# Attention by blocks of queries, with each block's end run as steps inside the next block

## The chip, the cores and the metric

One core of one Trainium2 chip. The metric is the time of one execution on the device, in microseconds (us). Each kernel was timed in several executions beside executions of the kernel before on the same chip. Later calls ran on different chips, so times are compared within a call, or by their ratio to the kernel before. A ratio is the mean time of one kernel's fast runs over the mean time of the other's fast runs of the same rounds, so it isn't quite the ratio of the medians that stand beside it. All timed runs of this study were of the fast state; a kernel with one single execution has no state that can be judged, and is marked so.

## The reference

Four images of 48 x 48 tokens with 128 channels go through two layers. The first is a selective scan (group norm, a projection, a 3 x 3 depthwise convolution with silu, scans in four directions, a gate and a projection). The second is what this change is about: attention over the 2304 tokens of an image, and a spectral convolution (`_stu`) of the normalised result.

```python
def _L1_attn_ref(x):
    attn = jnp.einsum('bnd,bmd->bnm', x / TEMPERATURE, x)      # TEMPERATURE = 1
    attn = jax.nn.softmax(attn, axis=-1)
    return jnp.einsum('bnm,bmd->bnd', attn, x)
...
t = _to_tokens(x)                                    # (4, 2304, 128)
t = t + _L1_attn_ref(_ln_t(t))
t = t + _L1_ffn_ref(_ln_t(t), ...)                   # spectral convolutions of the second norm
```

## The kernel before

The four images are handled one after the other ("batches" 0 to 3). Each has three stages:

- the **scans**: 768 of them, VectorE's and GpSimd's work, and beside them on TensorE the spectral convolutions (`cv`) of the batch before;
- the **turn**: the scans' epilogue, then the attention, with the next batch's prologue (projections `ip` on TensorE, 18 depthwise "taps" of 2.6 us on VectorE, silu on ScalarE) put between its steps;
- the **tail**, run as the first steps of the next batch's scans: the attention's result is turned, divided by the softmax's denominators, added to the tokens `T`, normalised into `u`, and stored for the convolutions. The convolutions can't start before it ends.

The attention goes over all keys, and for each over five chunks of queries, so that five accumulators end together. ScalarE's exponential also adds up the denominators:

```python
for i in range(NT + 1):                                        # 18 blocks of 128 keys
    nxt = pool.two.tile([P, L], F32, tag="e", ...) if i < NT else None
    for q, (lo, w) in enumerate(chunks):                       # 4 x 512 and 1 x 256 queries
        if i < NT:
            p = ps.pss.tile([P, 512], F32, tag="s", ...)
            nc.tensor.matmul(p[:, :w], xnT[:, i * P:(i + 1) * P], xnT[:, lo:lo + w], start=True, stop=True)
            nc.scalar.activation(nxt[:, lo:lo + w], p[:, :w], AF.Exp, bias=shift, accum_out=sm[:, i, q:q + 1])
        if i > 0:
            values(i - 1, e, q)
        yield
    e = nxt
```

The norm that closes the tail visits four engines' queues in turn, which matters below:

```python
def normed(x, d, eps, small, sq, name):
    ...
    nc.vector.tensor_tensor(d, x, s.unsqueeze(2).to_broadcast([k, m, C]), ALU.subtract)   # u <- T
    nc.scalar.activation(sq[:k], d, AF.Square)                                            # usq <- u
    yield
    nc.vector.tensor_reduce(v, sq[:k], AX.X, ALU.add)
    nc.vector.tensor_scalar(v, v, 1.0 / C, eps, ALU.mult, ALU.add)
    nc.gpsimd.tensor_tensor(v, v, mhalf[:k, :m], ALU.pow)                                 # ln_vu
    yield
    nc.vector.tensor_tensor(d, d, v.unsqueeze(2).to_broadcast([k, m, C]), ALU.mult)       # u <- u, ln_vu
```

Scans and convolutions are interleaved by a count of matmul columns. `more` puts convolutions down until their share of the columns has caught up with the scans' share; each of the tail's steps is booked in that count with 300 columns, 4500 in all:

```python
def more(share):
    while done[0] < share * total:         # total: the scans' own columns + work_cols
        cols = next(work, None)
        if cols is None:
            break
        done[0] += cols
...
TAIL_COLS = 300
TAIL_COLS_ALL = TAIL_COLS * (NM + 10)      # 4500
...
scans(b, *first, front, sp, ps, later(b - 1, held, ps), STU_COLS + TAIL_COLS_ALL)
```

## Time and profile before

| what | kernel before |
|---|---|
| time, median of 3 runs | 7205.91 us (7194.62 to 7206.78) |
| TensorE busy, share of the span | 88% |
| VectorE, GpSimd, ScalarE | 67%, 53%, 42% |
| mean granted clock of TensorE | 0.911 |

How to read it: TensorE bounds two of the three stages, and its 88% is an average over those and over two holes, the epilogue and the tail. The prediction shows the stretches. Two more lines are needed later. The first is from the page's table of groups: busy us and mean ns of one, then the idle time of the engine just ahead of them and what ended most of it.

```profile
L698 PE MATMUL s<-xnT 128*128 128x512 f32 (+1 forms) x720 | 340.3, 556 | 2.0 <-ACT e L699 2.0
```

The second is the largest entry of TensorE's waits in the first attention with prologue (1298 to 1470 us), a step of the scans' preparation: us in total, times, longest.

```profile
PE sp L395 <- ACT u L378: 2.0, 1, 2.0
```

So before, a score hardly ever waits for an exponential: 2.0 us in the whole program.

### The profile page before, as it was taken

To read this page: it belongs to the slowest core of one execution; us is meant where nothing else is said; L and a number is where in the kernel's file an instruction comes from. 1 tells how busy PE (TensorE), PEld (TensorE's weight loads), DVE (VectorE), ACT (ScalarE), POOL (GpSimd) and SP (SyncE) were. 2 spreads that over 40 slices of the span, in tenths; PEclk is the share of its full clock that TensorE was granted. 3 is DMA by queue.
4 is the path that set the end of the run, shared out by engine and by line. 5 is a ranking of instruction groups with operands and counts; after the bars stand their busy time and mean duration, and the time that the engine had idled before them with its cause. 6 is when DMAs were issued, how large, how long until landed. Compare 5 with 4: busy or idle time off the path is not lost. (4 is left out here: it accounts for less than half of the span.)

```text
span 7207.2 us, 79853 instructions
## 1 busy us (share of the span) xinstructions
PE 6362.3 (88%) x26760; PEld 3677.8 (51%) x26760; DVE 4834.5 (67%) x6045; ACT 3028.8 (42%) x5984; POOL 3837.3 (53%) x1795
## 2 busy tenths in 40 slices
PE   4777776868999998878999999778999999889999
PEld 2333333434555566534555556534555556547788
DVE  6899887467888876447888886447888887412111
ACT  3666664434444543334445543344444543231000
POOL 2888886046777775025677775215677776300000
PEclk7777777989999999889999999889999999789999
DMA  4555553056767676045767776126767777215545
GB/s 96 135 138 133 139 136 95 15 122 144 180 178 187 182 192 178 14 96 130 178 173 186 184 191 199 39 62 134 168 170 182 188 187 200 72 35 139 157 142 176
DMA packets 648924, 1019.14 MB, mean 141 GB/s; under 512 B 93850, under 2 KB 506650, under 8 KB 623779
## 3 DMA queue, kind: packets, MB, share of 16 engines
q1 hardware_dynamic: 642816, 1010.84, 54.6%
q8 instruction: 213, 3.49, 0.2%
q10 hardware_dynamic: 5698, 3.21, 0.2%
q14 instruction: 197, 1.61, 0.1%
HBM read 895.86 MB, written 117.84 MB: 141 GB/s over the span
## 5 line engine op out<-in xcount | busy, mean ns | idle before, releaser
L456 POOL TENSOR_TENSOR s<-s,bc 128x1536 f32<-128x1536 f32 x768 | 2645.9, 3446 | 259.3 <-DVE s L447 156.7
L447 DVE TENSOR_TENSOR_SCAN s<-dA,carry,s 128x384 f32<-128x384 f32 x2560 | 2437.8, 999 | 229.5 <-ACT dA L444 222.0
L444 ACT ACTIVATE dA<-rep,A 128x384 f32<-128x384 f32 x3072 | 1753.8, 584 | 991.4 <-DVE s L447 976.2
L948 PE MATMUL cv<-tt,u 128*128 128x256 f32 (+4 forms) x7680 | 1684.2, 359 | 84.5 <-DVE U L968 71.4
L948 PEld LDWEIGHTS cv<-tt,u 128*128 128x128 f32 (+1 forms) x7680 | 1276.5, 191 | 669.0 <-issue 298.6
L968 DVE TENSOR_TENSOR U<-cv,Q 128x256 f32<-128x256 f32 (+1 forms) x1280 | 490.8, 391 | 1116.9 <-PE cv L948 1100.3
L439 POOL TENSOR_TENSOR s<-rep,bc 128x1536 f32<-128x1536 f32 x288 | 993.9, 3451 | 98.1 <-DMA bc<-bcd 98.1
L948 PE MATMUL cv<-tt,us 128*128 128x256 f32 (+4 forms) x3840 | 870.1, 363 | 88.5 <-DVE U L968 39.4
L439 DVE TENSOR_TENSOR s<-rep,B 128x1536 f32<-128x1536 f32 x480 | 833.9, 1737 | 72.1 <-PE B L431 58.6
L464 PE MATMUL y<-s,csum 128*32 128x384 f32 x6144 | 718.2, 542 | 168.3 <-POOL s L456 155.1
L957 ACT COPY Q<-cv 128x256 f32<-128x256 f32 (+3 forms) x640 | 224.5, 351 | 1410.3 <-PE cv L948 1288.6
L948 PEld LDWEIGHTS cv<-tt,us 128*128 128x128 f32 (+1 forms) x3840 | 638.6, 192 | 342.9 <-issue 142.0
L1006 PE MATMUL pr<-U,G 128*128 128x512 f32 (+4 forms) x2048 | 733.9, 492 | 47.9 <-DMA G<-gd 43.3
L455 POOL COPY carry<-s 128x4 f32<-128x4 f32 x640 | 120.3, 188 | 1191.4 <-DVE s L447 1123.0
L447 DVE TENSOR_TENSOR_SCAN s<-dA,s 128x384 f32<-128x384 f32 x512 | 457.3, 939 | 52.1 <-ACT dA L444 48.7
L431 PE MATMUL B<-xd,spread 32*128 32x384 f32 x960 | 473.7, 575 | 18.8 <-DVE s L439 18.1
L1006 PEld LDWEIGHTS pr<-U,G 128*128 128x128 f32 x2048 | 348.3, 198 | 261.7 <-issue 174.9
L464 PEld LDWEIGHTS y<-s,csum 128*32 128x32 f32 x6144 | 126.0, 112 | 598.8 <-POOL s L456 294.4
L161 POOL TENSOR_TENSOR ln_vu<-ln_vu,mhalf 128x4 f32<-128x4 f32 (+1 forms) x20 | 20.1, 1005 | 762.2 <-DVE ln_vu L160 762.2
L699 ACT ACTIVATE e<-s,shift 128x512 f32<-128x512 f32 (+1 forms) x360 | 232.0, 644 | 304.8 <-PE s L698 303.8
L698 PE MATMUL s<-xnT 128*128 128x512 f32 (+1 forms) x720 | 340.3, 556 | 2.0 <-ACT e L699 2.0
L809 PE MATMUL G<-M,W 128*128 128x128 f32 (+2 forms) x768 | 237.7, 459 | 116.6 <-DMA M<-in_M_phi_plus 114.9
(165 smaller groups left out, 5055.5 us busy)
## 6 DMA issues: line engine op xcount, KB each, us to landing
rep<-dtdud SPq DMA_DIRECT2D x768, 384.0 KB, 7.8
tt<-fd SPq DMA_DIRECT2D x192, 577.0 KB, 4.1
bc<-bcd SPq DMA_DIRECT2D x2304, 48.0 KB, 3.8
tt<-fd SPq DMA_DIRECT2D x192, 513.0 KB, 4.1
tt<-fd SPq DMA_DIRECT2D x192, 385.0 KB, 4.0
dtdud<-re SPq DMA_DIRECT2D x768, 96.0 KB, 2.2
G<-gd SPq DMA_DIRECT2D x192, 256.0 KB, 4.8
tt<-fd SPq DMA_DIRECT2D x64, 514.0 KB, 5.4
```

The source lines that it names most:

```text
L431: nc.tensor.matmul(self.bt[:, :CS], spread[32:64, self.q].rearrange("p c j -> p (c j)"), self.ch.xd[32:64], start=True, stop=True)
L439: eng.tensor_tensor(s, self.ch.rep[self.h][:, 1], bt.unsqueeze(1).to_broadcast([P, G4, CS]), ALU.mult)
L444: nc.scalar.activation(dA[:, :CS], ch.rep[self.h][:, 0, g], AF.Exp, scale=A[:, ch.k, self.h * G4 + g, self.q:self.q + 1])
L447: nc.vector.tensor_tensor_scan(s, dA[:, CS - 1::-1] if ch.rev else dA[:, :CS], s, 0.0 if ch.first else carry[:, self.h, self.q, g:g + 1], ...
L456: nc.gpsimd.tensor_tensor(self.s, self.s, ch.bc[Q4 + self.q].unsqueeze(1).to_broadcast([P, G4, CS]), ALU.mult)
L464: nc.tensor.matmul(ch.y[g * DL:(g + 1) * DL, :CS], csum, self.s[:, g], start=(self.q == 0), stop=(self.q == Q4 - 1))
L698: nc.tensor.matmul(p[:, :w], xnT[:, i * P:(i + 1) * P], xnT[:, lo:lo + w], start=True, stop=True)
L699: nc.scalar.activation(nxt[:, lo:lo + w], p[:, :w], AF.Exp, bias=shift, accum_out=sm[:, i, q:q + 1])
L809: nc.tensor.matmul(p[:, :n] if j else p[:, NF - 1 - i], W[:, q if t else 0, i], M[t][:, i].unsqueeze(1).to_broadcast([P, n, C]) if j else ...
L948: nc.tensor.matmul(p2[:, :, at - first:], x, t[:kp, :, hi - 1 - at + J * P:end if end >= 0 else None:-1], start=(J == 0), stop=(J == nb - 1))
L968: nc.vector.tensor_tensor(dst, src, q, ALU.add)
L1006: nc.tensor.matmul(p[:, :, :v], Gs[n][:, q, x, :], U[n][:, 4 * q:4 * q + 4, :v], start=False, stop=(k == KF - 1 and q == 1 and v == w))
```

## The change

Its intent: let the attention finish a block of 512 queries at a time, so that the tail of a block can run as single steps inside the next block, and only one block's tail is left when the scans start. Parts:

1. Loops exchanged: blocks of queries in the order 0, 4, 1, 2, 3 outside, keys inside. Scores of a block can start as soon as pieces of `xnT` are kept, so they start within the epilogue.
2. The denominators: the last channel of the values' operand is set to 1, so the values matmul itself gives the sum of the exponentials there. The true last channel is got back as minus the sum of the others, since the rows of `xn` have mean 0.
3. Each block's tail is a generator, stepped once per attention step.
4. The tail and its 4500 columns leave the scans.

```diff
-    def attention(b, xn, xnT, oT, den, pool, ps):
...
+        pieces = [0, 4, 1, 2, 3]
+        slots = [(J, i) for J in pieces for i in range(NT)]
+        es, po, tails = [], {}, []
...
+        for J, i in slots:
+            w = P * PIECES[J]
+            p = ps.two.tile([P, 512], F32, tag="mu", name=f"s{b}_{J}_{i}")
+            nc.tensor.matmul(p[:, :w], xnT[:, i * P:(i + 1) * P], xnT[:, 512 * J:512 * J + w], start=True, stop=True)
+            e = pool.four.tile([P, 512], F32, tag="e", name=f"e{b}_{J}_{i}")
+            nc.scalar.activation(e[:, :w], p[:, :w], AF.Exp, bias=shift)
+            es.append((J, i, e))
+            if len(es) > 2:
+                values()
+            if tails and next(tails[0], True):
+                tails.pop(0)
+            yield
...
+    def tail(b, J, T, po, pool, ps):
+        ...
+        nc.vector.tensor_copy(oT[:, :P * n], po[:, :P * n])
+        yield
+        ...                                     # transposes otr
+        nc.vector.tensor_copy(r, p[:, :, C - 1])
+        nc.vector.reciprocal(r, r)
+        nc.vector.tensor_reduce(s, p[:, :, :C - 1], AX.X, ALU.add)
+        nc.vector.tensor_tensor(s, s, r, ALU.mult)
+        yield
+        ...                                     # added to T, stored, normed, turned (utr), kept (uT), stored
...
             nc.scalar.copy(xnT[:, at(J)], pt.pop(J)[:, :P * PIECES[J]])
+            nc.gpsimd.memset(xn[:, 4 * J:4 * J + PIECES[J], C - 1:], 1.0)
...
-            scans(b, *first, front, sp, ps, later(b - 1, held, ps), STU_COLS + TAIL_COLS_ALL)
+            scans(b, *first, front, sp, ps, stu_alone(b - 1, ps), STU_COLS)
...
+        at = attention(b, T, xn, xnT, back, back, ps)
+        slots = NT * len(PIECES)
+        for i, J in enumerate(epilogue(b, T, xn, xnT, turn.one, back, ps)):
             if i % 2 and parts:
                 parts.pop(0)()
+            if J is not None:
+                for _ in range(PIECES[J]):
+                    next(at)
+                    slots -= 1
```

## The prediction

> **What bounds the kernel now.** I read the page's slices first, which show four repeats of one pattern, then cut the span at the stage borders with the view of stretches, then followed the borders in order of time. Each of the four batches has: the scans (beside them, on TensorE, the convolutions `cv` of the batch before; in batch 0 a lighter mixture), the scans' epilogue, the attention (beside it the next batch's prologue), and the tail (attention's result turned, divided, added to T, normalised into u and stored). The last batch's convolutions run alone. Columns: stretch, its length, then busy us (count) of PE, PEld, DVE, ACT, POOL, then the clock, DMA share, GB/s.
>
> ```profile
> 1203.00:1298.00 95.00, 67.25 (x259) 54.24 (x252) 46.41 (x106) 18.33 (x31) 18.76 (x17) 0.70 0.15 50
> 1298.00:1470.00 172.00, 165.68 (x430) 79.62 (x428) 55.68 (x30) 88.75 (x226) 0.00 (x0) 1.00 0.17 42
> 1470.00:1519.00 49.00, 14.05 (x45) 7.91 (x44) 37.11 (x67) 13.40 (x23) 18.14 (x11) 0.53 0.25 70
> 1600.00:2700.00 1100.00, 1054.87 (x4655) 595.75 (x4648) 904.91 (x1087) 526.48 (x996) 784.49 (x359) 0.98 0.70 177
> 6285.00:6427.00 142.00, 141.70 (x360) 68.46 (x359) 1.48 (x3) 68.87 (x184) 0.00 (x0) 0.99 0.00 0
> 6427.00:6460.00 33.00, 7.51 (x38) 5.29 (x38) 21.82 (x56) 5.69 (x11) 5.03 (x5) 0.58 0.31 87
> 6460.00:7207.00 747.00, 735.37 (x3460) 582.21 (x3460) 129.57 (x325) 59.00 (x165) 0.00 (x0) 0.99 0.52 153
> ```
>
> The attention is bound by TensorE: alone (fifth row) it takes 142 us at full clock, with the prologue's matmuls 172. The scans with convolutions are bound by TensorE too (96% busy, against DVE's 82%). The holes are the epilogue and the tail: 49 us with TensorE busy for 14 in batches 0 to 2, and 33 with 7.5 in batch 3. Those are what the change aims at. The borders:
>
> ```profile
> 1290.16 0.59 ACT L661 COPY xnT<-xtr 128x512 f32<-128x512 f32 x1
> ...
> 1298.74 3.02 PE L698 MATMUL s<-xnT 128*128 128x512 f32 x6
> ```
>
> ```profile
> 1476.50 1.79 DVE L447 TENSOR_TENSOR_SCAN s<-dA,s 128x384 f32<-128x384 f32 x2
> ...
> 1511.55 1.80 DVE L447 TENSOR_TENSOR_SCAN s<-dA,s 128x384 f32<-128x384 f32 x2 [1.80 <-ACT dA L444]
> ...
> 1519.04 2.05 PE L948 MATMUL cv<-tt,us 128*128 128x256 f32 x4 [8.94 <-DMA tt<-fd]
> ```
>
> The first piece of xnT is ready 8 us before the first score: all that an overlap of epilogue and attention can win is there, since earlier than that no score has its operand. And during the tail the scans advance by only some 2.5 of 192 units (four scans of a unit in pairs), where the later pace is (2863-1523)/189.5 = 7.07 us a unit.
>
> [...] the taps, 2.6 us each, run back to back, and DVE idled for 20.45 us ahead of the copy `oT` until TensorE's last values came. So what counts for a step put between others is the program's order. [...] I take rates from starts (512 columns of f32: 0.86 us, two records 0.43 apart).
>
> **The change part by part.** I built both orders of instructions and compared them.
>
> (1) Attention by blocks: the same 90 score and 90 value matmuls with the same widths and weight loads, so nothing is won or lost on TensorE. The 90 accumulator reads of ScalarE go (17.4 us of 0.193 in the first attention), but ScalarE is busy for 89 of 172 us and idle waiting for the scores: worth 0.
>
> (2) Earlier start: 18 of the 90 steps follow each kept piece, from 1290.8 instead of 1298.7: -8.0. But what TensorE did there must still run: four projections of 0.82 (14.7 us over 18) and fourteen transposes of 0.13 (18 took 2.39): +5.2. Net -3.
>
> (3) The tails of blocks 0, 4, 1, 2 in the attention: 28 full transposes x 0.13 = +3.7 on TensorE. On DVE a block of four costs about 8 us (copy 0.69, reciprocals and sum 1.0, four additions 1.2, norm 1.6 + 0.9 + 0.7, sums 0.4, small ones), five of them 36 us beside the 56 of the prologue: 92 of about 190, which looks harmless, but
>
> (4) the order makes it bite. In the new order the copy of block 0's result stands ahead of all 18 taps, so taps that ran at 1301 now wait for block 0 to end (about 1334). And the prologue's parts are spread over 90-18-25 = 47 steps instead of 70. Near block 1's end stand six taps: from `oT` to the u that TensorE must turn, DVE has 0.7 + 5.2 + 1.0 + 2.6 + 1.4 + 2.6 + 3.2 + 2.6 + 0.7 = 20.0 us, while TensorE's seven steps and the transposes need 12.6: a stall of 7.5. Then the second silu, after a last tap, holds the next batch's first projection: 2.5. Block 0's tail lies in the narrow block (steps of 0.86 us): DVE 14.8 against TensorE's 12: 3. Pieces kept and scores in turn, ScalarE between, partly at half clock: 4. Sum: +17. The 6 us of idle time at the scans' preparation stay.
>
> So an attention with prologue ends -3 + 3.7 + 17 = about +18 later.
>
> (5) What is left of the tail is one block. From its last values to uT: copy 0.9, transposes 0.75, denominators 1.2, additions 1.35, norm 1.6 + 0.75 + 0.9 + 1.15 + 0.85, transposes 0.85, copy 0.8 = 11. Then the queue: the store of u stands before the loads of `tt`, and in the last tail of before 7.0 us passed from the end of the last uT copy to the first `cv` (6453.6 to 6460.6). So `cv` starts 18 us after attention instead of 49 (33.7 in batch 3): -31. Of the scans, before did in its 49 us about 4 us of TensorE's work that is now still to come: +4. The 4500 columns booked for the tail leave the count by which scans and convolutions are interleaved, and its transposes leave the scans; that is in the start's difference already. Net -27.
>
> Sum: batches 0 to 2: 18 - 27 = -9 each, -27. Batch 3 has no prologue, so no taps: start -4.7, transposes +1.9 and +3.7, stalls about +9 (half clock 4, block 0's tail in the narrow block 3, block 4's trip through memory 2): +10; its tail 18 instead of 33.7: -15.7; net -6. Total -33: 7206 - 33 = 7173 us.
>
> **The rivals.** (a) The stalls of (4) don't come, because ScalarE and DVE have slack after all: for it speaks DVE's 32% in the attention, against it the order. Then each batch wins about 26, the last 12: -90, 7115 us. (b) DVE becomes the bound in the stretch of the taps, and waits in its FIFO for ScalarE's squares, GpSimd's powers (1.01 us) and the reload of block 4 delay the taps further: stalls of 35 instead of 17 a batch, and the gain at the start is paid out: +20, 7226 us. (c) The gain at the scans' start is not real because DVE paces the scans, and 2.5 units must be caught up at 5.6 us (batch 0's pace, 1081/192): against it TensorE's 96%. Then the start wins 17 instead of 27: 7203 us. (d) Values now lag two steps behind scores instead of five: in the narrow block 1.7 us for a score (0.43), an exponential (0.47) and two handovers of 0.2 to 0.35; a copy of z (0.47) between makes it late. Some 5 us more per batch, 7193.
>
> **Range and chances.** The two terms of 17 to 18 and 27 to 31 pull against each other in each of three batches; an error of 20 us in either moves the sum by 60. Between (a) with a little more (7110) and (b) with a little more (7235) I put 8 chances in 10. Two per cent would be 144 us, some 40 per batch: even with no stall at all it would need more than the 49 us of the tail to vanish; and to lose as much, stalls of 65 us per batch. Faster 0.04, within 0.93, slower 0.03.
>
> **What would show it.** The span from the first score to the last value: about 198 us instead of 171 in batches 0 to 2, some 155 instead of 142 in batch 3; the first score about 8 us earlier, 5 in batch 3. DVE's taps in two groups, the second around block 1's tail, and TensorE idle before `utr` with DVE's u named, 5 us and more once per batch. From the last value to the first `cv` 18 us; from attention's end to the last product of the scans about 1366 us instead of 1393. If the attention stays at 180 us or less, (4) is wrong; if the first `cv` comes later than 25 us after attention, the queue's order in (5) is wrong; if the scans' stage doesn't shorten while `cv` starts earlier, (c) is right. A scan stage that needs more than 7.1 us a unit would be something that I have not seen.

## The result, and the profile after

| | median (range), runs | ratio to the kernel before, 95% interval |
|---|---|---|
| before | 7203.47 us (7194.62 to 7206.78), 4 | |
| after | 7141.64 us (7139.91 to 7153.94), 4 | 0.992, 0.9903 to 0.9937 |

62 us less at the medians, where 33 were predicted; inside 2%, and inside the predicted range. Two more calls gave ratios of 0.9939 and 0.9943 (below).

I cut each trace at four events of each batch: the first mean of the epilogue (start of the turn), the first score, the end of the last value, and the first `cv`. The next batch's first mean ends the stage of the scans; for batch 3 that is the end of the program. The two profiled executions differ by 66.3 us, in these places (us):

| stretch | before: batches 0, 1, 2 | after: batches 0, 1, 2 | before: 3 | after: 3 |
|---|---|---|---|---|
| first mean to first score | 94.9, 94.3, 92.3 | 86.7, 86.9, 87.9 | 76.4 | 72.0 |
| first score to last value | 171.4, 171.7, 171.7 | 201.5, 201.5, 201.6 | 142.1 | 153.6 |
| last value to first `cv` | 48.9, 49.3, 49.0 | 20.9, 20.6, 21.0 | 33.7 | 17.7 |
| first `cv` to the stage's end | 1346.0, 1355.9, 1359.1 | 1342.8, 1348.7, 1332.5 | 746.6 | 744.5 |

The turns grow, the wait for the first `cv` shrinks by more than half, and the rest of the scan stage shrinks too. The view of stretches of the kernel after, for batch 0's turn and tail, answers to the first three rows that the prediction shows (columns as there: PE, PEld, DVE, ACT, POOL, clock, DMA share, GB/s):

```profile
1200.50:1287.20 86.70, 58.33 (x234) 49.26 (x230) 43.74 (x100) 14.81 (x23) 16.27 (x16) 0.72 0.16 54
1287.20:1488.80 201.60, 181.54 (x480) 87.36 (x480) 80.05 (x102) 86.95 (x149) 9.91 (x10) 0.95 0.18 48
1488.80:1509.70 20.90, 4.96 (x13) 2.14 (x13) 13.91 (x21) 3.81 (x6) 4.39 (x2) 0.61 0.23 55
```

In the attention (second row) TensorE is now idle for 20 us of 201.6, and its clock is 0.95 instead of 1.00. The group table shows that scores now wait, 51.8 us in the whole program instead of 2.0, most of it for exponentials; and that the same 720 records of scores take 15.7 us more, 580 ns each instead of 556, which goes with the lower clock:

```profile
L700 PE MATMUL s<-xnT 128*128 128x512 f32 (+1 forms) x720 | 356.0, 580 | 51.8 <-ACT e L702 28.5
```

TensorE's waits in batch 0's attention (1287.2 to 1488.8 us), the longest entries:

```profile
PE s L700 <- ACT e L702: 9.3, 3, 5.2
PE s L700 <- ACT xnT L662: 4.4, 2, 3.7
PE utr L865 <- DVE u L163: 3.7, 2, 3.1
```

The first and the third entry are the waits at the ends of blocks 0 and 1, 13.0 us together. Of the second, the wait of 3.7 us stands ahead of the first score, so it isn't part of the attention's 201.6 us; inside it the scores wait for pieces of `xnT` for 0.7 us.

The wait of 5.2 us, in order of time. The lines are from the timeline of the kernel after: start, duration, engine, line and operation, and in brackets the idle time of that engine ahead of it and what ended that. "..." leaves out scores, values and exponentials that run as usual, and small operations of VectorE:

```profile
1398.42 0.68 DVE L832 COPY oT<-o 128x512 f32<-128x512 f32 x1
1399.03 5.26 DVE L266 SCALAR_TENSOR_TENSOR xc<-xpad,cw,xc 128x2304 f32<-128x2304 f32 x2
...
1405.26 2.61 DVE L266 SCALAR_TENSOR_TENSOR xc<-xpad,cw,xc 128x2304 f32<-128x2304 f32 x1
...
1407.79 1.12 DVE L846 SCALAR_TENSOR_TENSOR T<-otr,den,T 128x127 f32<-128x127 f32 x4
...
1408.89 2.61 DVE L266 SCALAR_TENSOR_TENSOR xc<-xpad,cw,xc 128x2304 f32<-128x2304 f32 x1
...
1412.34 0.69 DVE L156 TENSOR_TENSOR u<-T,ln_su 128x512 f32<-128x512 f32 x1
1413.06 0.63 ACT L157 ACTIVATE usq<-u 128x512 f32<-128x512 f32 x1 [7.53 <-DVE u L156]
1413.60 1.25 ACT L702 ACTIVATE e<-s,shift 128x512 f32<-128x512 f32 x2
...
1414.32 2.07 PE L700 MATMUL s<-xnT 128*128 128x512 f32 x2 [5.22 <-ACT e L702]
...
1414.52 2.61 DVE L266 SCALAR_TENSOR_TENSOR xc<-xpad,cw,xc 128x2304 f32<-128x2304 f32 x1
1414.76 3.24 POOL L161 TENSOR_TENSOR ln_vu<-ln_vu,mhalf 128x4 f32<-128x4 f32 x1 [34.24 <-DVE ln_vu L160]
...
1418.78 0.66 PE L865 MATMUL utr<-ident,u 128*128 128x128 f32 x4 [0.68 <-DVE u L163]
1419.27 1.02 PE L700 MATMUL s<-xnT 128*128 128x512 f32 x2
```

Read it from VectorE: block 1's result is copied at 1398.42, but taps stand between the tail's steps, and `u` (less its mean) isn't ready before 1413.03. ScalarE's queue has the `Square` of that `u` ahead of the next exponentials. It idles for 7.53 us; two scores stand finished in the two PSUM buffers and wait for their exponentials; and TensorE idles for 5.22 us for a buffer. The stall of block 1 is where it was predicted, but its gate is ScalarE, one norm step before `utr`. After it, two records of scores take 2.07 us where they took 1.02: half the clock. The granted clock was 0.50 from 1414.3 to 1418.0, and 0.96 in the 4 us after that. Block 1 has one more wait, of 2.06 us at 1423.22: there the exponential stands behind the prologue's second silu (`th<-xc`), for which ScalarE idled 6.91 us until the last tap was done.

Then the start of the scans in batch 1, from the timeline of the kernel after:

```profile
1488.80 0.69 DVE L832 COPY oT<-o 128x512 f32<-128x512 f32 x1 [17.55 <-PE o L693]
...
1495.88 1.01 POOL L161 TENSOR_TENSOR ln_vu<-ln_vu,mhalf 128x4 f32<-128x4 f32 x1 [25.81 <-DVE ln_vu L160]
1496.85 3.42 POOL L439 TENSOR_TENSOR s<-rep,bc 128x1536 f32<-128x1536 f32 x1
1496.92 3.90 DVE L163 TENSOR_TENSOR u<-u,ln_vu 128x512 f32<-128x512 f32 x1 [1.18 <-POOL ln_vu L161]
...
1500.96 1.08 PE L865 MATMUL utr<-ident,u 128*128 128x128 f32 x4 [10.75 <-DVE u L163]
...
1509.69 2.08 PE L939 MATMUL cv<-tt,us 128*128 128x256 f32 x4 [2.58 <-DMA tt<-fd]
```

From the last block's copy to the first `cv` there are 20.9 us, and one line in it is odd: VectorE's product `u<-u,ln_vu` takes 3.90 us. It has 20 such products in the program, of 676 ns at the least and 693 at the median. Here it started while GpSimd ran its first large product of the scans, 1496.85 to 1500.27, and it ended 0.55 us after that. The loss is 3.2 us; experiment 7 asks whether GpSimd's product is the reason. The mirror of it is in the timeline above: GpSimd's power at 1414.76, of four elements a partition, took 3.24 us where the one at 1495.88 took 1.01; a tap of VectorE, 1414.52 to 1417.13, ran beside it, and the power ended 0.87 us after the tap.

### The profile page after: what moved, and what is told of

Its sections match the earlier page's. It is cut to its first block, busy times and chain, and to the rows that moved or that the text cites. A ratio compares the mean times of both kernels' runs of the same rounds, so it can differ in the third digit from the quotient of the medians.

```text
span 7140.9 us, 79677 instructions
## 1 busy us (share of the span) xinstructions
PE 6335.6 (89%) x26760; PEld 3652.2 (51%) x26760; DVE 4863.0 (68%) x6145; ACT 2986.6 (42%) x5616; POOL 3849.3 (54%) x1815
## 5 line engine op out<-in xcount | busy, mean ns | idle before, releaser
L997 PE MATMUL pr<-U,G 128*128 128x512 f32 (+4 forms) x2048 | 717.6, 482 | 48.7 <-DMA G<-gd 40.5
L700 PE MATMUL s<-xnT 128*128 128x512 f32 (+1 forms) x720 | 356.0, 580 | 51.8 <-ACT e L702 28.5
L693 PE MATMUL o<-e,xn 128*128 128x512 f32 (+1 forms) x720 | 340.2, 556 | 0.0
```

The costliest lines, as they stand in the source:

```text
L693: nc.tensor.matmul(po[J][:, :w], xn[:, i], e[:, :w], start=(i == 0), stop=(i == NT - 1))
L997: nc.tensor.matmul(p[:, :, :v], Gs[n][:, q, x, :], U[n][:, 4 * q:4 * q + 4, :v], start=False, stop=(k == KF - 1 and q == 1 and v == w))
```

## The experiments

My theory, in three parts: the attention is longer as predicted, since VectorE's order of taps and tail steps makes someone wait; the first `cv` lost 3 us to the product that ran beside GpSimd's (3.90 us instead of 0.69); and the scans' further gain comes from the convolutions' lead, that is from the 4500 columns, which I had not counted as a gain of their own (I came to this one after the first call). Rivals: the further gain is scatter between executions; the loss in the turn comes from the overlap with the epilogue, or from a part of the attention that I had written off as free (the denominators).

### 1. The same two kernels again

No edit. Both are run once more, to see how much of each stage is scatter.

> The changed kernel unaltered, to see how far its stages repeat. In its first profile the three scan stages that carry convolutions took, from the attention's last value to the first mean of the next epilogue, 1363.7, 1369.4 and 1353.5 us, against 1394.8, 1405.1 and 1408.2 before: -31, -36 and -55 where the prediction's step 5 had -27 each. Theory (a): only the scans' start is shorter (its first eighth of a chunk series, -36), and the rest of the differences, about -20 in the third scan, is scatter between executions: then the three stages of this run are again 1350 to 1375, the third not always the shortest, the whole within 15 us of 7142. Theory (b): the third scan is truly faster by 20 us and more for a reason of the program (layout of buffers, interleaving): then it repeats within 3 us.

> The kernel before unaltered, one look, for the same question. Theory (a), scatter: its scan stages with convolutions differ from 1394.8, 1405.1 and 1408.2 by up to 15 us in either direction. Theory (b): they repeat within 3 us. In both its attention turns (first mean to last value) repeat at 266, 266, 264 and 218.5 us within 2 us, since nothing there waits for a long transfer.

After: 7157.7 us (7156.19 to 7158.45) against 7196.21 (7192.44 to 7217.32) of before in the same call, ratio 0.9939 (0.9924 to 0.9954). Before, a single execution: 7190.56 us, state unknown. A third time, in a later call:

> The changed kernel unaltered once more, beside the two that follow on the same chip, so that they can be compared in time. Turns 288 to 290 and 226 us as twice before, scan stages with convolutions 1350 to 1377, the whole 7140 to 7160.

7150.89 us (7144.6 to 7164.16) against 7194.45, ratio 0.9943 (0.9923 to 0.9963). By stage (us, batches 0, 1, 2):

| | turn (first mean to last value) | last value to first `cv` | first `cv` to the stage's end |
|---|---|---|---|
| before | 266.3, 266.0, 264.0 | 48.9, 49.3, 49.0 | 1346.0, 1355.9, 1359.1 |
| before again | 266.2, 265.8, 268.1 | 49.8, 48.5, 48.5 | 1348.6, 1345.9, 1348.0 |
| after | 288.2, 288.3, 289.5 | 20.9, 20.6, 21.0 | 1342.8, 1348.7, 1332.5 |
| after again | 288.1, 289.2, 289.7 | 21.3, 20.9, 21.1 | 1355.2, 1344.9, 1337.8 |
| after, third | 288.2, 289.6, 289.9 | 21.0, 20.6, 21.1 | 1351.6, 1345.1, 1329.2 |

The turn and the wait for the first `cv` repeat to 2 us, but for the third turn of before (264.0 and 268.1). The rest of the scan stage scatters by over 10 us. So neither theory about the third stage holds as it was put: it is the shortest of the three in every profile of after, but it doesn't repeat within 3 us. Cut at scans 64, 160, 320, 640 and 736, the scatter sits in the stretch from 640 to 736: that takes 186 to 187 us where the granted clock was 0.982 and 203 where it was 0.89. Means over six such stages of before and nine of after: 1350.6 and 1343.1. So the 62 us of the first call were at the good end; three calls gave differences of the medians of 62, 38.5 and 43.6.

### 2. Without the overlap of epilogue and attention

```diff
         for i, J in enumerate(epilogue(b, T, xn, xnT, turn.one, back, ps)):
             if i % 2 and parts:
                 parts.pop(0)()
-            if J is not None:
-                for _ in range(PIECES[J]):
-                    next(at)
-                    slots -= 1
```

> Blocks and tails as in the changed kernel, but no step of attention within the epilogue: all 90 steps follow it, and the prologue's parts are spread over 65 steps, not 47. My theory: the overlap gives almost nothing net. First score about 95 us after the first mean instead of 86.7 (+8), but the taps start again before block 0 has ended and run ahead, so TensorE's stalls fall from about 14 us beyond those at the scans' preparation to about 6, and four projections leave the attention (-4): each turn of batches 0 to 2 within 5 us of the changed kernel's 288 us; batch 3, without prologue, +5: the whole within 15 us of 7142. The rival, that the overlap is what pays: +8 in every turn and no stall less, so +30 us, about 7172.

7134.2 us (7128.85 to 7137.91), 0.9906 (0.989 to 0.9922), against after's 7157.7 in the same call: 23 us faster. The turns are 282.3, 281.3 and 282.5 us: the first score comes 7.2 us later than in the kernel after of the same call (94.6 instead of 87.4 on average), and the attention is 14.2 us shorter (187.4 instead of 201.6). So the overlap is a net cost of 7.0 us per turn; the prediction had it at nearly nothing. In batch 3, where I expected 5 us more, the turn is 225.0 us, no longer than after's. TensorE's waits in that attention (1295 to 1484 us):

```profile
PE s L700 <- ACT e L702: 6.2, 2, 3.5
PE utr L865 <- DVE u L163: 1.7, 2, 1.3
```

The 0.7 us of waiting for kept pieces (`xnT`) are gone, and the waits at the blocks' ends are 7.9 instead of 13.0 us. The view of stretches over this attention, to be held against the second row of after's:

```profile
1295.60:1483.20 187.60, 173.97 (x459) 83.92 (x457) 77.48 (x94) 82.29 (x141) 5.56 (x4) 0.97 0.19 51
```

Of the 14 us that the overlap costs in the attention, TensorE's idle time is 6.4 (20.1 instead of 13.6; 5.1 of it at the blocks' ends) and its busy time 7.6 (181.5 instead of 174.0), of which the prediction had 5.2 as moved transposes and projections. In the trace of the kernel after, the overlapped steps ran at a clock of 0.81 (1287.2 to 1300), here the attention's first 13 us had 0.98. This run also spreads the prologue's parts over 65 steps instead of 47; so what of the shorter waits at the blocks' ends is the overlap and what the spread, this run alone doesn't tell.

What is left, 282.0 us against before's 266.1, is the cost of blocks and tails alone: 15.9 us per turn, in the first attention 8.8 us more busy time of TensorE and 7.3 more idle time.

### 3. The denominators as before

```diff
-            nc.scalar.activation(e[:, :w], p[:, :w], AF.Exp, bias=shift)
+            nc.scalar.activation(e[:, :w], p[:, :w], AF.Exp, bias=shift, accum_out=sm[:, n:n + 1])
```

The kernel after, with the sums of the exponentials taken again (and thrown away).

> The changed kernel with the accumulator output of the exponential put back (its sums go to a tile that nobody reads; the result stays right). It adds 90 reads of 0.19 us per batch on ScalarE, 17 us, where ScalarE idles for more than half of the attention. My theory (step 1 of the prediction): worth nothing, at most 1 us a batch in the narrow block, the whole within 6 us of 7142. The rival: that the denominators' new place is what pays, because the two-step lag leaves no room in ScalarE's queue: then +10 us and more per batch, 7180 and above.

7162.46 us (7146.83 to 7169.8), 0.9949 (0.993 to 0.9968), beside after's 7157.7. The turns are 291.3, 293.3, 291.4 and in batch 3 225.6: 2 to 4 us longer in the batches with a prologue, nothing in batch 3. The part is worth nearly nothing, though not the 0 of the prediction: where ScalarE's queue gates TensorE, its accumulator reads count.

### 4. The tail's Square two steps later

If the stall of block 1 comes from ScalarE waiting for `u` ahead of its exponentials, then putting the `Square` two steps later must take it away, unless the wait moves.

```diff
         nc.vector.tensor_tensor(d, x, s.unsqueeze(2).to_broadcast([k, m, C]), ALU.subtract)
+        for i in range(late):                                  # 2 for the tail's norms
+            yield
         nc.scalar.activation(sq[:k], d, AF.Square)
```

> The changed kernel with the tail's square (ScalarE) issued two steps later than the subtraction (VectorE) that it needs. In the changed kernel TensorE's longest stalls in the attention stand before scores (5.2 us in block 1's tail, 2.0 in block 0's), waiting for an exponential that stands behind the tail's square in ScalarE's queue, which waits for VectorE, which is at the taps. Theory (a), the square in ScalarE's queue is what turns VectorE's delay into a stall: those two gaps shrink to under 1 us, each turn of batches 0 to 2 falls from 288 to 289 us to about 282, batch 3 from 226 to 225, the whole to about 7138 on the scale of the last run (7158). Theory (b), VectorE's work itself is the bound there, and the wait only moves to the transposes of u: the gap before them grows from 0.7 and 3.1 us to 5 and more, and the turn stays within 2 us of 288.

7148.47 us (7137.59 to 7150.19), 0.993 (0.9903 to 0.9957), where the kernel after had 0.992 to 0.9943. The turns: 288.1, 289.5, 289.4, the same as after's to half a microsecond. TensorE's waits in batch 0's attention:

```profile
PE s L702 <- ACT e L704: 7.2, 1, 7.2
PE utr L867 <- DVE u L165: 5.6, 1, 5.6
```

12.8 us at the blocks' ends, where the kernel after had 13.0. Block 0's wait for an exponential (2.0) became wait for `u` (3.1 to 5.6). Block 1's came in one piece: in this trace ScalarE still idles for 4.07 us until `u` is ready for the `Square`, and then for 4.55 more until the taps are done that the prologue's silu needs, and the exponential stands behind both. So the `Square`'s place alone isn't the cause; VectorE's queue, with taps between the tail's steps, is, and it hands the wait to whichever queue asks next. What the silu's place in ScalarE's queue costs by itself, no run tests. Only batch 3, with no taps, gained: 223.3 instead of 225.5 us.

### 5. The prologue's parts within the overlapped steps

```diff
             if J is not None:
                 for _ in range(PIECES[J]):
                     next(at)
+                    if parts:
+                        parts.pop(0)()
                     slots -= 1
```

> The changed kernel with one more part of the next batch's prologue after each of the 18 steps that lie in the epilogue, so that the projections are done and the taps begin before block 0 ends, and the rest is spread at 1.4 instead of 1.8 parts per step. My theory of step 4 (the taps pile up behind block 0's result, VectorE idles for 29 us before it): stalls fall by some 8 us per turn of batches 0 to 2, to about 280 us, as without the overlap but with the 8 us kept; the whole about 7132 on the scale of 7158. The rival: taps in the epilogue stand ahead of its own norms in VectorE's queue, so the pieces are kept later: first score to last value no shorter than 201 us, the turn 288 or more.

7142.51 us (7135.55 to 7162.53), 0.9925 (0.9901 to 0.9949). Turns 283.9, 286.8 and 286.8: 2 to 4 us shorter, where I expected 8. The waits at the blocks' ends (TensorE's gaps in batch 0) are 1.1 + 3.1 for block 0 and 2.5 + 2.6 for block 1, 9.4 in all instead of 13.0. The attention is 3 to 4 us shorter for it (197.3, 198.5 and 197.7), and the first score isn't later. So part of what the overlap costs is that fewer steps are left for the same parts. In the whole time the gain is inside the scatter of the scans.

### 6. The 4500 columns, booked again

The kernel after, with the count of columns as it was before: a step that does nothing is booked with 4500 columns at the start of the convolutions.

```diff
+        yield 4500
...
-            scans(b, *first, front, sp, ps, stu_alone(b - 1, ps), STU_COLS)
+            scans(b, *first, front, sp, ps, stu_alone(b - 1, ps), STU_COLS + 4500)
```

> The changed kernel with 4500 columns booked at the start of each scan stage for work that isn't there, as the kernel before booked them for its tail, so that the convolutions lie behind the scans by as much as before. It asks why the scan stage between its 64th and its 320th scan got shorter, by 8 and 5 us, at a higher granted clock (0.94 to 0.98, and 0.99 to 1.00). Theory (a): how convolutions and scans lie against each other sets how often TensorE's clock is halved: the 64th to 160th go back to about 181 us at a clock of 0.93 to 0.95, the 160th to 320th to about 273. Theory (b): it has another cause: they stay at 171 to 176 and 266 to 269 us.

A single execution: 7182.07 us against 7202.88 of before in that call, state unknown. From first `cv` to the stage's end it took 1351.2, 1356.9 and 1353.1, mean 1353.7, where the kernel after has 1343.1 (nine stages) and before 1350.6 (six). These totals alone wouldn't prove it: the means of the seven other versions without the columns (one execution each, three stages) lie between 1339 and 1352. But the two stretches that theory (a) named both went back: scans 64 to 160 take 177.4 to 183.0 us (after 170.2 to 176.8, before 176.4 to 182.6), and scans 160 to 320 271.6 to 277.6 (265.9 to 272.4, and 271.4 to 275.2). Its reason isn't shown: the clock of scans 64 to 160 did fall (0.94 to 0.97 instead of 0.97 to 0.99), but the stage changes at full clock too. The evidence that doesn't depend on scatter is the stretch from scan 320 to 640, at full clock in nearly all runs. In batch 1's stage, the view of stretches of the kernel before, of this run, and of the kernel after, in that order:

```profile
2098.20:2614.20 516.00, 507.03 (x2251) 292.00 (x2250) 437.75 (x514) 259.75 (x484) 391.48 (x176) 1.00 0.71 183
```

```profile
2087.00:2603.00 516.00, 507.00 (x2251) 291.94 (x2250) 437.84 (x513) 259.80 (x484) 391.43 (x176) 1.00 0.71 183
```

```profile
2082.00:2594.00 512.00, 504.67 (x2244) 289.76 (x2243) 437.95 (x514) 257.40 (x482) 390.21 (x176) 1.00 0.71 185
```

With the columns booked, the stretch is that of the kernel before to a tenth of a microsecond; without them it is 4 us shorter (511.4 to 514.7 in after's nine stages, 516.0 to 516.2 in before's six), and TensorE has 7 fewer matmul records in it. The last stretch of the stage, after scan 736, goes from 62.6 (also in the kernel before) to 60.4 us in the same way. Where the missing work went, by the number of `cv` records in each stretch of batch 1's stage:

| from first `cv`, cut at scan | 64 | 160 | 320 | 640 | 736 |
|---|---|---|---|---|---|
| before | 112 | 232 | 496 | 1120 | 700 |
| booked | 112 | 232 | 496 | 1120 | 700 |
| after | 124 | 244 | 495 | 1106 | 704 |

24 more run in the first 160 scans, where TensorE had about 20 us idle in the first 64 alone; the first two stretches take 304.9 us on average with the columns booked (three stages) and 307.9 without (nine), 3 us for work of 24 x 0.36 (the mean of a `cv` record) = 8.6. The rest of it seems to have been moved from a place where TensorE is the bound to one where it isn't. This is the step that I had missed.

### 7. A candidate: no overlap, a later Square, and ScalarE scales the last block

To test what the slow product costs at the start of the scans, the last block's product by `ln_vu` goes from VectorE to ScalarE; the two other edits are those of 2 and, for all blocks but the last, of 4.

```diff
+        if act:                                                # the last block's norm
+            for j in range(m):
+                nc.scalar.activation(d[:, j], d[:, j], AF.Copy, scale=v[:, j:j + 1])
+            return
         nc.vector.tensor_tensor(d, d, v.unsqueeze(2).to_broadcast([k, m, C]), ALU.mult)
```

> Blocks and tails, without the overlap, with the late square, and in the last block's tail the scaling of u by the deviation on ScalarE (four instructions) instead of VectorE, where in the changed kernel that multiplication takes 3.9 us instead of 0.7, because GpSimd started a 3.4 us multiplication for the scans just before. Theory: the turn of batches 0 to 2 falls from 282 (without overlap) to about 277, and the first convolution comes about 18 us after the last value instead of 20.9, in batch 3 no change (17.7, GpSimd is idle there): together 8 us per batch less than without overlap, about 7112 on the scale of 7134. The rival, that GpSimd is not what lengthens it: first convolution still at 20 to 21 us.

7133.17 us (7118.36 to 7150.55), 0.9909 (0.9877 to 0.9941). The first `cv` comes 17.6, 17.2 and 18.0 us after the attention instead of 20.9, in the time that batch 3 needs in the kernel after (17.7), where no scans stand beside the tail; with only one of the two other edits it was 20.6 to 21.3. So the 3 us of the slow product are shown. That GpSimd's product beside it is the reason agrees with a line that stayed on VectorE: the sum `us<-u`, 0.43 us alone, took 2.34 at 1497.44 and ended 0.28 us after GpSimd's product (1496.07 to 1499.50). How the one holds up the other, no run shows. The line that replaces the product of 3.90 us, from this kernel's timeline:

```profile
1496.14 1.28 ACT L167 ACTIVATE u<-u,ln_vu 128x128 f32<-128x128 f32 x4 [2.11 <-POOL ln_vu L163]
```

The other half of the theory failed: the turns are 282.3, 284.1 and 283.8 us, not 277, so the later `Square` gains nothing here either. The whole isn't faster than experiment 2 (7134.2, another call). In the profiled execution, the slowest of the four, the scan stages were 1350.5 to 1354.3 us, at the upper end.

### 8. Where the prologue's parts must end

`BEGIN` is the number of attention steps that are kept for the scans' preparation; the prologue's parts are spread over the steps ahead of it. A larger one moves all taps earlier, and so away from block 1's tail. Both runs leave the overlap out and scale on ScalarE; the Square is at its old place.

```diff
-    BEGIN = 25
+    BEGIN = 36          # the other run: 45
```

> Blocks and tails, no overlap, the last block's scaling on ScalarE, and the next batch's scans prepared over the last 36 steps instead of 25, so that the prologue's parts lie on 54 steps: no tap stands behind block 1's result any more, and only a few behind block 0's. It tests what is left of step 4: that the place of the taps against the blocks' ends in VectorE's queue makes the stalls, the late square having shown that the square's place in ScalarE's queue doesn't. Theory (a): the 3.7 us stall in block 1's tail goes, block 0's shrinks from 4.7 to about 3, the turn falls from 282 to 277 or 278, the first convolution at 17.6 us: whole about 22 us under the changed kernel by the turns and 10 by the first convolutions, some 7120 to 7125 where that has 7150. Theory (b), VectorE's own work in the tail (8 us a block, beside steps of 0.86 us) makes them wherever the taps are: turn 281 to 284.

> The same with the preparation over the last 45 steps and the parts on 45: all taps of the first half stand ahead of block 0's result, those of the second half in the narrow block 4's tail and before block 1's. Theory (a): block 0's stall falls below 2 us, block 1's is gone, block 4's may rise to 2; turn 276 to 279. Theory (b): 281 to 284, as in begin36.

At 36: 7116.09 us (7106.95 to 7131.61), 0.9896 (0.9872 to 0.9921); at 45: 7126.14 (7117.85 to 7133.6), 0.9906 (0.9888 to 0.9924); beside them after's 7150.89. The version with 36 is the fastest of the study, and its range lies wholly below that of the kernel after in the same call. But its turns, 280.1, 281.7 and 282.4, are hardly shorter than those of experiment 2 (theory (a) had 277 to 278), and those at 45, 285.0, 283.7 and 285.7, are longer than either theory had. So its lead over the kernel after is nearly all the overlap left out and the earlier first `cv`, not `BEGIN`. Two of TensorE's waits in batch 0's attention (1298.9 to 1486.1 us), and the longest one from the timeline, show why:

```profile
PE ip L247 <- ACT xpad L256: 5.9, 4, 4.4
PE utr L869 <- DVE u L167: 2.0, 1, 2.0
```

```profile
1345.74 0.63 ACT L157 ACTIVATE usq<-u 128x512 f32<-128x512 f32 x1 [4.37 <-DVE u L156]
...
1346.64 0.47 ACT L256 COPY xpad<-ip 128x384 f32<-128x384 f32 x1
...
1347.16 1.65 PE L247 MATMUL ip<-xT,win 128*128 128x384 f32 x2 [4.35 <-ACT xpad L256]
```

Block 1's wait is gone. Block 0's is still there under another name: a projection of the prologue waits for the copy `xpad<-ip`, and that copy stands in ScalarE's queue behind the `Square` of block 0, which idles for 4.37 us until `u` is ready. The 2.0 us at `utr` are block 4's. At 45 the two longest gaps are 3.9 us at a copy `oT` behind taps and 6.7 us at a score whose exponential stands behind the prologue's silu, both at block 4's end. The wait moves with the taps, wherever these runs put them.

### 9. Still further ahead

If a lead of the convolutions is worth time, more of it might be worth more. The fastest version, with the first 4500 columns of the convolutions left out of the count:

```diff
-        yield from stu(b, pool, ps)
+        ahead = AHEAD                                          # 4500
+        for cols in stu(b, pool, ps):
+            free = min(cols, ahead)
+            ahead -= free
+            yield cols - free
...
-            scans(b, *first, front, sp, ps, stu_alone(b - 1, ps), STU_COLS)
+            scans(b, *first, front, sp, ps, stu_alone(b - 1, ps), STU_COLS - AHEAD)
```

> The mirror of the run with 4500 phantom columns, on the version that starts its steps at scan 36 and leaves the overlap out: here the first 4500 columns of the convolutions are not counted, so that the convolutions run about 6 scans further ahead. Theory (a), that the convolutions' lead is worth its columns: scans 320 to 640 of each scan stage fall from about 512.5 to about 509 us, the stage from first convolution to next first mean falls by up to 9 us each, and the whole comes to 7085 to 7105 us where the version without it had 7116. Theory (b), that the start cannot take more: the first 64 scans grow by as much as the rest loses (134 to about 142 us), because the first convolutions must wait for their loads and the clock is below 1 there, and first convolution to next mean stays at 1335 to 1350 us, the whole at 7110 to 7125.

7173.85 us (7171.5 to 7193.95), 0.9957 (0.9941 to 0.9974): slower than without (0.9896), by far more than theory (b) allowed for. From first `cv` to the stage's end: 1371.8, 1372.1 and 1362.9, where the version without it has 1342.7, 1335.5 and 1342.4. Two of the first three stretches of batch 1's stage (to scan 64, and from 160 to 320), the version with `BEGIN` 36, then this one:

```profile
1503.50:1637.20 133.70, 112.50 (x396) 54.32 (x397) 92.83 (x122) 54.79 (x108) 72.75 (x37) 0.90 0.60 141
1807.00:2074.40 267.40, 261.17 (x1133) 144.96 (x1132) 228.62 (x272) 133.72 (x251) 195.12 (x88) 0.99 0.70 177
```

```profile
1499.80:1651.00 151.20, 126.08 (x428) 61.85 (x428) 95.56 (x129) 56.20 (x111) 74.89 (x37) 0.88 0.54 128
1827.90:2104.70 276.80, 260.61 (x1120) 142.70 (x1119) 226.28 (x271) 131.72 (x250) 193.86 (x88) 0.99 0.69 170
```

Theory (a)'s stretch came as it said: scans 320 to 640 fell from 514.5 to 508.7 us. But the first stretch grew by 17.5 us for 13.6 of TensorE's busy time, so it had no room left; the second (to scan 160) grew by 7.1 at a clock of 0.96 instead of 1.00; and the third, with 13 records fewer, grew by 9.4. There the convolutions wait longer for VectorE's additions into `U`, which free their PSUM buffers. TensorE's waits in that stretch, the version with `BEGIN` 36, then this one:

```profile
PE cv L943 <- DVE U L963: 4.7, 6, 1.4
```

```profile
PE cv L943 <- DVE U L963: 15.6, 11, 2.6
```

So more lead isn't always better: of the three leads tried (on two versions of the kernel), the middle one was the best, and the change had moved towards it by luck. Why the third stretch waits more, when its convolutions are only shifted, I haven't shown.

## Why the prediction was right or wrong

The time was inside the range and the class was right, and the mechanism is the predicted one: the attention pays, the start of the scans gains more. The size came out of terms whose errors partly cancel: the turn and the first `cv` each came some 3 to 5 us later than predicted, and a gain that the prediction hadn't counted made up for it. Without that one (10.6 us per stage, below) the sum of all terms would have been about -19 (an estimate from the table), not -51. Means of the profiled runs, two of before and three of after (in the first two rows one of each, so that they don't quite add up to the third), us per batch of batches 0 to 2:

| term of the prediction | predicted | measured |
|---|---|---|
| first score earlier | -8 | -6.7 (93.8 to 87.2) |
| attention longer (5.2 + 3.7 + 17) | +26 | +29.9 (171.6 to 201.5) |
| turn, the sum of the two | +18 | +22.9 (266.1 to 289.0) |
| first `cv` after the attention | -31 | -28.0 (49.0 to 20.9) |
| rest of the scan stage | +4 | -7.5 (1350.6 to 1343.1) |
| sum per batch | -9 | -12.6 |

Three of these sums make -38, batch 3 adds -11 (predicted -6): its turn grew by 6.8 instead of 10, its tail shrank by 15.9 as predicted (15.7), and its convolutions took 1.8 less. With 2 us of scatter in the first scans that is -51, against medians of -62, -38.5 and -43.6 in three calls.

Step (1), denominators and accumulators worth 0: nearly. Taking the sums again cost 2 to 4 us per turn with a prologue, nothing in batch 3 (experiment 3).

Step (2), "Net -3" for the overlap, with 4 more for its stalls in step (4), so +1: **mis-sized**. It is +7.0 (experiment 2). The 8 us were there, 7.2 in that pair of runs; what came back was 14.2 us instead of 9. The prediction's stalls at the kept pieces are small in the trace (gaps of 0.6 and 0.7 us inside batch 0's attention; the 3.7 us at `xnT` stand ahead of the first score), but the overlapped 12.8 us ran at a clock of 0.81, which is some 2.4 us more (an estimate from the two). What was not foreseen are the 5.1 us that the waits at the blocks' ends gain by the overlap; by experiment 5, part of that comes from the fewer steps that are left for the same parts.

Steps (3) and (4), transposes 3.7 and stalls of 13 at the blocks' ends: the stalls are right in size. In the kernel after, the gaps at the blocks' ends are 5.0 us for block 0 (predicted 3) and 8.0 for block 1 (predicted 10, of which 2.5 at the silu; 2.1 came there), and TensorE's idle time in the attention grew by 13.7 us (6.4 to 20.1). Its busy time grew by more than was predicted, 16.4 us (165.1 to 181.5) instead of 8.9 for transposes and projections; the lower clock, 0.95 instead of 1.00, goes with that. The named wait was wrong: I expected TensorE at `utr` with VectorE's `u` named, and it stood mostly at a score, with ScalarE's exponential named, behind a `Square` that waited for the same chain of VectorE. Experiment 4 shows that for block 0 the two are one wait: moving the `Square` turned one into the other. Experiments 5 and 8 show that it follows the taps, shrinking by some microseconds but never leaving. Rival (a), no stalls, fell with this. So did rival (b): VectorE is busy for 40% of the attention (80.05 of 201.6 us), and the idle time grew by 13.7 us, not 35. It is no bound; its order is what costs. That an engine works in the order of the program was an assumption under step (4); the trace of after agrees with it where ScalarE idled for 7.53 us ahead of the `Square` while two finished scores waited for their exponentials. Rival (d), a lag of two steps for 5 us, has no trace: apart from the gaps named and the scans' preparation, TensorE has none above 0.4 us in the first attention. One reading of the prediction is off without consequence: during the tail the scans advance by 8, which is 2 units and not 2.5.

Step (5), first `cv` 18 us after the attention: 20.9, and 17.0 to 18.0 once the product beside GpSimd's scan was moved to ScalarE (experiments 7 and 8), as in batch 3 (17.7). The chain was added up rightly, and one of its links, 0.7 us long when alone, took 3.9 beside another engine's work.

Step (5), last sentence, **failed**: "The 4500 columns booked for the tail leave the count ...; that is in the start's difference already." It isn't. With them booked again, the rest of the stage took 1353.7 us, 3.1 more than before, close to the +4 that I had put down for undone scan work; without them 1343.1. So the count is worth some -10.6 us per stage on its own (a single execution on one side of this difference and scatter of the same size, but with the stretches from scan 64 to 640 as before). I had looked at what the booked columns stood for, and not at what they do: they set how far ahead of the scans the convolutions run. Rival (c), the gain at the start isn't real, fell: the stage did shorten with the earlier `cv`, and by more.

Open: the third scan stage of the kernel after is shorter than the first two in all three profiles, by 7 to 22 us, and not so in the two of before. The difference goes with the granted clock in the last block of convolutions (0.982 in stretches of 186 to 187 us, 0.89 in one of 203, experiment 1); why the clock is higher there I don't know.

## What to carry to other kernels

When a tail is cut into steps and woven into another stage, list for each engine's queue what stands ahead of what: here the wait followed VectorE's chain of long taps and short tail steps through every rearrangement, and the cheapest cure that these runs found was to weave less (leave the overlap out), not more. A count that steers an interleaving is a tuning value of its own: when a change alters it in passing, test it alone, since here 4500 columns, 0.7% of the stage's work, were worth about 10 us per stage, and another 4500 cost 20 to 37. And look for a short link of a critical chain that runs beside something long on a neighbour: here the product of 0.69 us took 3.90 on VectorE beside GpSimd's product of 3.42, and the four scalings that replaced it took 1.28 on ScalarE beside the same kind of product, and brought the first `cv` 3 us earlier.

## What these traces showed of the hardware

- VectorE and GpSimd side by side: a product of 0.69 us on VectorE took 3.90 beside a GpSimd product of 3.42, once per scan stage and on the critical chain, and a power of four elements a partition on GpSimd, 1.01 us alone, took 3.24 beside a tap of 2.61; on ScalarE four scalings took 1.28 us beside a GpSimd product of 3.43 (experiment 7).
- TensorE's clock after gaps, in the first attention of the kernel after: the gap of 5.22 us was followed by a clock of 0.50 from 1414.3 to 1418.0 us. Two shorter gaps, 1.98 and 3.05 us, with 1.13 us of work in between, were followed by a clock of 0.50 from 1342 to 1345 us.
- In an order of instructions steered by a count, one of three leads of the one stream over the other was the best: 1353.7 us per stage with 4500 columns more in the count, 1343.1 without, and 1368.9 (against 1340.2 in the version that it was tried on) with 4500 fewer.
